# Mamba-2 block with a LoRA feed-forward layer: x's transposes, D-skip, the decay scan and the layer norm get other places in their engines' order

## Chip, cores and metric

One core of one Trainium2 chip runs the whole program in one launch. The metric is the device time of that launch in microseconds (us); lower is better. The engines are TensorE (PE; PEld is its weight load), VectorE (DVE), ScalarE (ACT), GpSimd (POOL) and SyncE (SP), whose queue issues the DMAs. Everything is float32.

## The reference, cut to what matters

x is 2048 tokens by 1024 channels. It is normalised, goes through a state-space layer and through a linear layer with a routed LoRA, and both results are added to it.

```python
xn = layernorm(x)                                   # over 1024 channels
proj = xn @ in_proj_w.T                             # gate 4096 | hbc 6144 | dt 64
conv = conv_bias + sum(pad[:, k:k+L] * conv_weight[:, k] for k in range(4))   # of hbc
xBC = silu(conv)                                    # x: 64 heads x 64, B and C: 8 groups x 128
dt_p = softplus(dt + dt_bias);  dA = exp(dt_p * -exp(A_log))
state = state * dA + dt_p * x (outer) B             # token by token
y = state . C + x * D                               # "D-skip"
y = y * rsqrt(mean(y*y over a group of 512) + eps) * norm_weight * silu(gate)
out = x + y @ out_proj_w.T + (xn @ W_base.T + b_base + top-2 LoRA of xn)
```

## The kernel before

All matrices have channels on partitions. The kernel works in three stages:

- **Fill** (about 0 to 195 us). The layer norm of the first 1024 tokens (`ln_first`), the small projections, dt and the decays (`small`), and the first products of `in_proj`.
- **Loop** (about 195 to 2130 us). 32 blocks b: two halves s of 1024 tokens (b 0 to 15 and 16 to 31), in each 8 groups g, in each two times 512 tokens. A block has four chunks c = 0 to 3 of 128 tokens; one chunk is one *slot* of the loop at line 1115. In every slot the state-space scan of one chunk is woven into the products of `in_proj`.
- **Rest** (2130 us to the end). The gate, the norm's scale and `out_proj`.

A *product* is 8 matmuls of 128x512 (one of seven products of a pair of weight tiles, in the manner of Strassen). `products(n, side)` (line 657) takes n of them from a stream and, after each, does an equal share of a list of small steps. TensorE's instructions keep the order in which the program issues them. So do, among themselves, those given to `pin` (line 96): each is put behind the last one pinned, on VectorE. All other instructions of VectorE and most of ScalarE's are ordered by the compiler's scheduler, which lets an instruction go ahead as soon as it believes that its inputs are there; ScalarE's moves (L740), xdd (L825), silu (L707, L723) and squares (L901) are held in program order. At run time each engine takes its instructions strictly as ordered.

A slot (lines 1115 to 1227) runs: first product with its steps; `scan_b` of this chunk; first step of `scan_a` of the *next* chunk; second product with its steps; second step of `scan_a`; third product with its steps; a fourth product in some slots; last step of `scan_a`. The four lists of steps are `parts[0]` to `parts[3]`. What matters of it:

- `scan_b` (834). TensorE: 16 matmuls **ps_y** (8 heads, each 64 rows of a bank) that take the mask product `dab` and the tokens' x as weights, and add to what ScalarE has put there; 8 matmuls **ps_e** (state times C); 2 matmuls **ps_st** from **xdd**. VectorE: `ecp` = ecp * ps_e (L863), y into `xg` = ecp + ps_y (L864), the state's sum (L878), all pinned. GpSimd scales the state (L85).
- `scan_a` (782), for the next chunk. Step 1: the decay scan `es` on VectorE (L791, pinned; one buffer, which xdd of the chunk before still reads). Step 2: TensorE's `ps_cb` (C times B, and B transposed), ScalarE's copies `cbm` and `bt` (L803, L805), then the **D-skip** (L812): four ScalarE instructions that write x * D into the bank of ps_y, once VectorE has read it for the chunk before (L864); then the **mask product** `dab` = es * cbm on VectorE (L817). Step 3: **xdd** on ScalarE, 8 instructions (L825).
- `conv` (694): ten steps for the next block. Per part (two tiles) one on ScalarE and two of three VectorE instructions each (L717, pinned). In c = 0, 1 and 2 the first three go into `parts[1]`, the second three into `parts[2]`.
- `turned` (729), x by token for the next block, in two times (k = 0, 1) 17 steps: 16 **moves** of 32 partitions on ScalarE (L740) and then one **transpose** of the whole on VectorE (L746) with the multiplication by dt (L753), both pinned. k = 0 serves chunks 0 and 1, k = 1 chunks 2 and 3. The steps per slot and list are in line 1163; the transposes come in `parts[1]` of c = 3 (k = 0) and of c = 1 (k = 1).
- `ln_next` (274), the layer norm of the second half's tokens, in four pieces; a piece runs through the first eight slots of each three blocks of b 0 to 11. `small` (340) of the piece follows, a step a slot, at the head of `parts[2]`. Their VectorE instructions are not pinned.
- In the second half, in c = 1, GpSimd adds the sums of the output weights (`out_sums`, four instructions at L85, named wo); VectorE does others of them in c = 3 (L938).

Before the loop, lines 1081 to 1092 do `conv` of block 0 beside 14 products, then the first 17 steps of `turned`, then `scan_a` of the first chunk.

Of the kernel before, what the change touches and what calls it, by code (L numbers as in the profile page):

```python
# [10 lines left out]
ALU = mybir.AluOpType  # L11
AX = mybir.AxisListType
# [3 lines left out]
H = 64  # L16
# [27 lines left out]
def mamba_lora_kernel(  # L44
# [229 lines left out]
    def ln_next(s, i):  # L274
# [9 lines left out]
        nc.vector.tensor_tensor(a, flat[:, 0:2, :], flat[:, 2:4, :], ALU.add)  # L284
        nc.vector.tensor_tensor(b, flat[:, 4:6, :], flat[:, 6:8, :], ALU.add)
        nc.vector.tensor_tensor(a, a, b, ALU.add)
        of = [a[:, 0, :], a[:, 1, :]]
# [4 lines left out]
        yield  # L292
        total = scratch("lsq")
        for h in range(2):
# [12 lines left out]
        for h in range(2):  # L307
            normal(flat[:, 4 * h : 4 * h + 4, :], std, ALU.mult)
            yield
# [4 lines left out]
        t4, t2 = (ev.tile([P, KH, Q], F32, tag="ev", name=f"t_{s}_{i}_{j}") for j in (4, 2))  # L314
        nc.vector.tensor_tensor(t1, b12, b11, ALU.subtract)
        nc.vector.tensor_tensor(t2, b22, t1, ALU.subtract)
        nc.vector.tensor_tensor(t4, b21, t2, ALU.subtract)
        t3 = ev.tile([P, KH, Q], F32, tag="ev", name=f"t_{s}_{i}_3")
        nc.vector.tensor_tensor(t3, b22, b12, ALU.subtract)
        yield  # L320
# [12 lines left out]
    def small(s, i, chunks, sm, home):  # L333
# [8 lines left out]
        def tile(what, shape):  # L342
# [10 lines left out]
        nc.vector.scalar_tensor_tensor(u, dt, -1.0, dt, ALU.mult, ALU.max)  # L353
        nc.scalar.activation(u, u, AF.Exp, scale=-1.0)
        nc.vector.tensor_scalar(dt, dt, 0.0, None, ALU.max)
        yield
        nc.vector.tensor_scalar(u2, u, 2.0, None, ALU.add)
        nc.vector.reciprocal(u2, u2)
        nc.vector.tensor_tensor(u, u, u2, ALU.mult)
        nc.vector.tensor_tensor(u2, u, u, ALU.mult)  # L360
        nc.vector.tensor_scalar(po, u2, 1.0 / 19.0, None, ALU.mult)
        for k in range(8, 0, -1):
            nc.vector.scalar_tensor_tensor(po, po, 1.0 / (2 * k + 1), u2, ALU.add, ALU.mult)
        nc.vector.scalar_tensor_tensor(po, po, 1.0, u, ALU.add, ALU.mult)
        dts = dt_of[s][:, chunks, :]
        nc.vector.scalar_tensor_tensor(dts, po, 2.0, dt, ALU.mult, ALU.add)

        at, ex = tile("at", [P, nch, H]), tile("ex", [P, nch, H])
        nc.vector.tensor_tensor(at, dts, na.unsqueeze(1).to_broadcast([P, nch, H]), ALU.mult)
        nc.scalar.activation(ex, at, AF.Exp)  # L370
# [29 lines left out]
        for c in range(nch):  # L400
            nc.vector.tensor_tensor_scan(
                run[:, c, :], da[:, c, :], zero.to_broadcast([H, Q]), 1.0, ALU.mult, ALU.add
            )


        nc.vector.memset(da[:, :, 0:1], 0.0)
        da_d = dram.tile([nch, H, Q], F32, tag=f"da_d_{n}", name=f"da_d_{n}")
# [11 lines left out]
        def best(src, name):  # L419
            m = lp.tile([P, nch, 1], F32, tag=f"m_{name}", name=f"m_{name}_{n}")  # L420
            nc.vector.tensor_reduce(m, src, AX.X, ALU.max)
            oh = lp.tile([P, nch, NE], F32, tag=f"oh_{name}", name=f"oh_{name}_{n}")
            nc.vector.tensor_tensor(oh, src, m.to_broadcast([P, nch, NE]), ALU.is_equal)
            nc.vector.tensor_tensor(oh, oh, rank_b, ALU.mult)
            f = lp.tile([P, nch, 1], F32, tag="first", name=f"first_{name}_{n}")
            nc.vector.tensor_reduce(f, oh, AX.X, ALU.max)
            nc.vector.tensor_tensor(oh, oh, f.to_broadcast([P, nch, NE]), ALU.is_equal)
# [4 lines left out]
        nc.vector.scalar_tensor_tensor(rest, oh1, -3.0e38, lg, ALU.mult, ALU.add)  # L432
        m2, oh2 = best(rest, "b")
        nc.vector.tensor_tensor(m2, m2, m1, ALU.subtract)
        nc.scalar.activation(m2, m2, AF.Exp)
        yield
        nc.vector.tensor_scalar(m1, m2, 1.0, None, ALU.add)
        nc.vector.reciprocal(m1, m1)
        nc.vector.tensor_scalar(m1, m1, SCALING, None, ALU.mult)
        nc.vector.tensor_tensor(m2, m2, m1, ALU.mult)  # L440
        nc.vector.tensor_tensor(oh1, oh1, m1.to_broadcast([P, nch, NE]), ALU.mult)
        nc.vector.tensor_tensor(oh2, oh2, m2.to_broadcast([P, nch, NE]), ALU.mult)
        nc.vector.tensor_tensor(oh1, oh1, oh2, ALU.add)
        for c in range(nch):
            hv = sm[:, c, H + NE :].rearrange("p (e r) -> p e r", r=RANK)
            nc.vector.tensor_tensor(
                hv, hv, oh1[:, c, :].unsqueeze(2).to_broadcast([P, NE, RANK]), ALU.mult
            )
# [222 lines left out]
    def steps(gen, n):  # L671

        return [lambda: next(gen, None) for _ in range(n)]
# [108 lines left out]
    def scan_a(s, g, half, c):  # L782
# [23 lines left out]
        if put_sums:  # L806
            put_sums()

        psy = ps_one.tile([P, 4, Q], F32, tag="y", name=f"ps_y_{n}")
        for j in range(4):  # L810
# [3 lines left out]
            )  # L814
        ms = dab
        masked[:] = [
            nc.vector.tensor_tensor(  # L817
                ms, es, cbm.unsqueeze(1).to_broadcast([P, HG, Q]), ALU.mult
            )
        ]  # L820
        yield
# [1025 lines left out]
```

## Time and profile before

| what | us |
|---|---|
| three runs, median (lowest to highest) | 3426.97 (3425.16 to 3427.97) |
| the profiled execution, its own time | 3425.95 |
| its span, first to last instruction | 3424.2 |
| TensorE busy in the span | 3316.1 |
| VectorE, ScalarE, GpSimd busy | 2564.5, 1674.2, 701.5 |
| mean granted TensorE clock | 0.989 |

The profile is of one execution. A line of a timeline gives the start, the duration, the engine, the line of the kernel, the operation, what it writes <- what it reads, the shapes and the count; in square brackets stands the engine's idle time before it and whose work ended it. Durations of matmuls include their way through the array, so that neighbours overlap: 8 matmuls of 128x512 show as 3.60 us and follow each other every 3.43. In a list of waits a line reads: engine, tile and line that waited, <- whom for, us in total, times, the longest.

The typical slot holds three products and lasts 13.6 to 14.05 us if TensorE does not wait; one with four lasts 17.0 to 17.5.

### The profile page before, as it was taken

The numbers are of one execution on the slowest core, as the hardware profiler recorded it, in microseconds if no ns is written. First come the engines' busy times: TensorE is split into PE (matmuls) and PEld (weight loads), VectorE is DVE, ScalarE is ACT, GpSimd is POOL, SyncE is SP. The second block draws the span as 40 slices with busy tenths as digits, with TensorE's granted clock in tenths as the row PEclk, the third lists the DMA queues.
The fourth block names the chain that finished last, engine by engine and source line by source line (L and its number), as shares of the span: only waits on it lengthen the run. The fifth ranks groups of instructions, "written<-read, shape, count | busy, mean of one in ns | idle before, by whom it ended". The sixth has DMA issues, their size and how long they took to land.

```text
span 3424.2 us, 40725 instructions
## 1 busy us (share of the span) xinstructions
PE 3316.1 (97%) x13509; PEld 2163.9 (63%) x13509; DVE 2564.5 (75%) x2873; ACT 1674.2 (49%) x4014; POOL 701.5 (20%) x483
## 2 busy tenths in 40 slices
PE   9989999999999999999999999999999999999999
PEld 7445554554554454455445545688888788888888
DVE  7378878988868889898878886477877666556554
ACT  2267776787686677777687765222222200000000
POOL 4122222222200021121212121355655100000000
PEclk9999999999999999999999999999999999999999
DMA  7546565665588988999888889578777887585644
GB/s 254 188 149 212 191 215 174 198 214 189 191 288 293 317 277 288 290 283 286 256 257 267 258 270 299 181 262 286 263 258 263 286 307 244 193 303 185 213 163 147
DMA packets 550818, 826.69 MB, mean 241 GB/s; under 512 B 36688, under 2 KB 266320, under 8 KB 547024
## 3 DMA queue, kind: packets, MB, share of 16 engines
q1 hardware_dynamic: 550608, 824.08, 73.2%
q8 instruction: 108, 1.77, 0.2%
q14 instruction: 102, 0.84, 0.1%
HBM read 564.88 MB, written 259.06 MB: 241 GB/s over the span
## 4 chain that ended last, share of the span: by engine, by line
PE 67%; DVE 15%; ACT 8%; DMA 6%; issue 3%; SPq 1%; POOL 0%; DVEq 0%; ACTq 0%; POOLq 0%
PE ps_x_w L81 8%; PE ps_x_x L81 8%; PE ps_x_z L81 6%; PE ps_a_w L81 5%; PE ps_y_w L81 5%; PE ps_a_x L81 5%; PE ps_y_x L81 5%; PE ps_a_z L81 4%; PE ps_y_z L81 4%; DVE xg L717 3%; ACT x_blocks L740 3%; PE ps_e L81 2%; PE ps_y L81 2%; DVE es L791 2%; PE ps_x_b L81 2%
## 5 line engine op out<-in xcount | busy, mean ns | idle before, releaser
L740 ACT COPY x_blocks<-xg 32x256 f32<-32x256 f32 x1024 | 411.5, 402 | 15.1 <-DVE x_by_token L746 0.9
L85 POOL TENSOR_TENSOR state<-state,tot 128x512 f32<-128x512 f32 x112 | 133.0, 1187 | 1104.8 <-PE ps_e L81 960.6
L717 DVE SCALAR_TENSOR_TENSOR xg<-raw_x,cw,xg 128x512 f32<-128x512 f32 x384 | 337.1, 882 | 15.0 <-ACT xg L710 9.9
L825 ACT ACTIVATE xdd<-x_by_token,es 128x64 f32<-128x64 f32 x1024 | 259.7, 335 | 114.6 <-DVE x_by_token L753 110.2
L81 PE MATMUL ps_x_w<-t,w 128*128 128x256 f32 x1344 | 305.1, 380 | 0.0
L791 DVE TENSOR_TENSOR_SCAN es<-dab,here 128x1024 f32<-128x1024 f32 x128 | 296.1, 2314 | 8.7 <-DMA dab<-da_d 4.7
L81 PEld LDWEIGHTS ps_x_w<-t,w 128*128 128x128 f32 x1344 | 256.3, 191 | 42.6 <-issue 8.0
L812 ACT ACTIVATE ps_y<-xg,dsk 128x128 f32<-128x128 f32 x512 | 189.0, 369 | 111.7 <-DVE xg L864 91.2
L1784 ACT COPY ps_x_w<-ps_a_w 128x512 f32<-128x512 f32 x28 | 16.0, 570 | 419.6 <-PE ps_a_w L81 419.6
L81 PEld LDWEIGHTS ps_y<-dab,x_by_token 128*64 128x64 f32 x2048 | 113.9, 140 | 157.4 <-issue 142.0
L81 PE MATMUL ps_a_w<-q,w 128*128 128x256 f32 x896 | 204.1, 381 | 2.5 <-DMA w<-w 2.5
L81 PE MATMUL ps_y<-dab,x_by_token 128*64 128x128 f32 x2048 | 144.9, 285 | 58.9 <-DVE x_by_token L753 30.2
L81 PEld LDWEIGHTS ps_a_w<-q,w 128*128 128x128 f32 x896 | 171.2, 191 | 26.4 <-DMA w<-w 2.9
L81 PE MATMUL ps_x_x<-op_again,s_x 128*128 128x512 f32 x384 | 175.6, 600 | 3.0 <-ACT s_x L533 2.0
L863 DVE TENSOR_TENSOR ecp<-ecp,ps_e 128x512 f32<-128x512 f32 x120 | 81.9, 683 | 127.6 <-PE ps_e L81 123.9
L81 PE MATMUL ps_a_x<-op_again,a_x 128*128 128x512 f32 x384 | 173.3, 594 | 0.0
L81 PE MATMUL ps_y_x<-op_again,s_x 128*128 128x512 f32 x384 | 173.1, 593 | 0.0
L81 PE MATMUL ps_x_x<-op,s_x 128*128 128x512 f32 x368 | 169.1, 603 | 3.2 <-ACT s_x L533 3.2
L717 DVE SCALAR_TENSOR_TENSOR bc<-raw_b,cw,bc 128x512 f32<-128x512 f32 x192 | 157.6, 829 | 17.9 <-ACT bc L710 14.8
L81 PE MATMUL ps_y_x<-op,s_x 128*128 128x512 f32 x368 | 169.1, 603 | 0.0
L817 DVE TENSOR_TENSOR dab<-es,cbm 128x1024 f32<-128x1024 f32 x128 | 158.4, 1237 | 14.1 <-ACT cbm L803 13.8
L81 PE MATMUL ps_a_x<-op,a_x 128*128 128x512 f32 x368 | 165.8, 593 | 0.0
(326 smaller groups left out, 6630.8 us busy)
## 6 DMA issues: line engine op xcount, KB each, us to landing
w<-w SPq DMA_DIRECT2D x196, 512.0 KB, 3.8
dab<-da_d SPq DMA_DIRECT2D x128, 512.0 KB, 6.0
w<-wo SPq DMA_DIRECT2D x112, 448.0 KB, 4.8
raw<-ev SPq DMA_DIRECT2D x192, 256.0 KB, 3.5
a_x<-in_w_in_dram SPq DMA_DIRECT2D x168, 256.0 KB, 4.5
ecp<-run_d SPq DMA_DIRECT2D x256, 128.0 KB, 5.1
y<-xg SPq DMA_DIRECT2D x64, 512.0 KB, 5.7
gy<-y SPq DMA_DIRECT2D x64, 512.0 KB, 6.5
```

The source lines that it names most:

```text
L81: tc.keep_in_program_order(nc.tensor.matmul(*args, **kw))
L85: ins = nc.gpsimd.tensor_tensor(*args)
L717: ins = nc.vector.scalar_tensor_tensor(dst[:, i, :], raw[:, i, k : k + TB], cw[:, ti, k : k + 1], dst[:, i, :], ALU.mult, ALU.add,)
L740: ins = nc.scalar.copy(blocks[32 * b : 32 * b + 32, :, :, i, :].rearrange("p c j r -> p j c r"), x[32 * i : 32 * i + 32, :, 2 * k : 2 * k ...
L791: ins = nc.vector.tensor_tensor_scan(es.rearrange("p h t -> p (h t)"), dab.rearrange("p h t -> p (h t)"), here, 0.0, ALU.mult, ALU.add,)
L812: nc.scalar.activation(psy[:, j, :], xg[:, j, cs], AF.Copy, scale=dsk[:, at : at + 1])
L817: nc.vector.tensor_tensor(ms, es, cbm.unsqueeze(1).to_broadcast([P, HG, Q]), ALU.mult)
L825: ins = nc.scalar.activation(xdd[:, h, :], xdt[:, h, :], AF.Copy, scale=es[:, h, Q - 1 : Q])
L863: pin(nc.vector.tensor_tensor(ecp, ecp, pse, ALU.mult))
L1784: nc.scalar.copy(px, pa)
```

## The change

Five edits:

1. `turned` keeps its 34 steps per block but spreads them anew (table `TURN`): in c = 2, 0, 4, 4, 4 steps for the four lists (before 0, 3, 4, 3); in c = 3, 4, 0, 1, 3 (before 3, 4); in c = 0 as before 2, 3, 3, 2; in c = 1, 3, 0, 1, 0 (before 3, 4). The moves of a k end with `parts[0]` of c = 3 or c = 1, and the transpose comes with `parts[2]`, behind the conv steps of that list.
2. In `scan_a` the mask product stands ahead of the D-skip, and a `yield` parts them: the D-skip comes after the third product instead of the second.
3. The decay scan (first step of `scan_a`) is issued ahead of `scan_b` instead of behind it.
4. The VectorE instructions of `ln_next` and `small` are pinned (`chain`), so that they stand in one order with conv, transposes and sums. In `ln_next` the additions of squares move behind later work, and there are two more `yield`s; the steps per slot follow.
5. The 14 last products of the fill also take the first 17 steps of `turned`; only three are left behind them.

```diff
+    class Chained:
+
+        def __getattr__(self, name):
+            call = getattr(nc.vector, name)
+            return lambda *args, **kw: pin(call(*args, **kw))
+
+    chain = Chained()
...
-    def normal(part, by, alu):
+    def normal(part, by, alu, engine=nc.vector):
-        nc.vector.tensor_tensor(
+        engine.tensor_tensor(
...
         total = scratch("lsq")
+        sqs = []
+
+        def add_up(*pairs):
+            for a, b in pairs:
+                chain.tensor_tensor(a, a, b, ALU.add)
+
         for h in range(2):
-            normal(flat[:, 4 * h : 4 * h + 4, :], mean, ALU.subtract)
+            normal(flat[:, 4 * h : 4 * h + 4, :], mean, ALU.subtract, chain)
+            if sqs:
+                add_up((total, sqs.pop()))
             for k in (4 * h, 4 * h + 2):
                 sq = ev.tile([P, 2, 2 * Q], F32, tag="ev", name=f"lsq_{s}_{i}_{k}") if k else total
                 nc.scalar.activation(sq, flat[:, k : k + 2, :], AF.Square)
                 if k:
-                    nc.vector.tensor_tensor(total, total, sq, ALU.add)
+                    sqs.append(sq)
             yield
+        add_up((total, sqs[0]), (total, sqs[1]))
+        yield
         ps = over_channels([total[:, 0, :], total[:, 1, :]], "aux", f"var_{s}_{i}")
         std = lp.tile([P, 2 * Q], F32, tag="lnstd", name=f"std_{s}_{i}")
         nc.scalar.activation(std, ps, AF.Sqrt, bias=eps, scale=1.0 / DM)
-        nc.vector.reciprocal(std, std)
+        yield
+        chain.reciprocal(std, std)
         yield
...
+        ms = dab
+        masked[:] = [
+            nc.vector.tensor_tensor(
+                ms, es, cbm.unsqueeze(1).to_broadcast([P, HG, Q]), ALU.mult
+            )
+        ]
+        yield
         psy = ps_one.tile([P, 4, Q], F32, tag="y", name=f"ps_y_{n}")
         for j in range(4):
             at = 4 * g + j
             nc.scalar.activation(
                 psy[:, j, :], xg[:, j, cs], AF.Copy, scale=dsk[:, at : at + 1]
             )
-        ms = dab
-        masked[:] = [
-            nc.vector.tensor_tensor(
-                ms, es, cbm.unsqueeze(1).to_broadcast([P, HG, Q]), ALU.mult
-            )
-        ]
         yield
...
-    products(14, steps(conv(*blocks[0]), 10))
+    turn = turned(*blocks[0])
+    c1, m1 = steps(conv(*blocks[0]), 1), steps(turn, 1)
+    products(14, (c1 * 6 + [lambda: None] + (c1 + m1 * 2) * 4 + m1 * 9))
...
-    turn = turned(*blocks[0])
-    for _ in range(17):
+    for _ in range(3):
         next(turn)
...
+    TURN = (2, 3, 3, 2), (3, 0, 1, 0), (0, 4, 4, 4), (4, 0, 1, 3)
...
-            side += steps(ln, {2: 1, 3: 1, 4: 1, 5: 2, 6: 1}.get(at, 0))
+            side += steps(ln, {2: 1, 3: 2, 4: 1, 5: 3, 6: 1}.get(at, 0))
...
-                for p, k in zip(parts, ((2, 3, 3, 2), (3, 4), (0, 3, 4, 3), (3, 4))[c]):
+                for p, k in zip(parts, TURN[c]):
                     p += steps(turn, k)
             products(1, parts[0])
+            next(a, None)
             scan_b(*blk, c)
...
             if second:
                 load_decays(*second)
-            next(a, None)
...
             products(1, parts[1])
             next(a, None)
             products(1, parts[2])
+            next(a, None)
             products(min(n - 3, 1), parts[3])
             next(a, None)
             do_put_off()
```

Left out are the lines in `ln_next` and `small` that only say `chain.` for `nc.vector.`.

More of the change, by code (lines that the diff above doesn't have):

```diff
@@ L283, in ln_next @@
         b = ev.tile([P, 2, 2 * Q], F32, tag="ev", name=f"half_{s}_{i}")
-        nc.vector.tensor_tensor(a, flat[:, 0:2, :], flat[:, 2:4, :], ALU.add)
-        nc.vector.tensor_tensor(b, flat[:, 4:6, :], flat[:, 6:8, :], ALU.add)
-        nc.vector.tensor_tensor(a, a, b, ALU.add)
+        chain.tensor_tensor(a, flat[:, 0:2, :], flat[:, 2:4, :], ALU.add)
+        chain.tensor_tensor(b, flat[:, 4:6, :], flat[:, 6:8, :], ALU.add)
+        chain.tensor_tensor(a, a, b, ALU.add)
         of = [a[:, 0, :], a[:, 1, :]]
@@ L293, in ln_next @@
         total = scratch("lsq")
+        sqs = []
+        def add_up(*pairs):
+            for a, b in pairs:
+                chain.tensor_tensor(a, a, b, ALU.add)
         for h in range(2):
-            normal(flat[:, 4 * h : 4 * h + 4, :], mean, ALU.subtract)
+            normal(flat[:, 4 * h : 4 * h + 4, :], mean, ALU.subtract, chain)
+            if sqs:
+                add_up((total, sqs.pop()))
             for k in (4 * h, 4 * h + 2):
@@ L304, in ln_next @@
         nc.scalar.activation(std, ps, AF.Sqrt, bias=eps, scale=1.0 / DM)
-        nc.vector.reciprocal(std, std)
+        yield
+        chain.reciprocal(std, std)
         yield
         for h in range(2):
-            normal(flat[:, 4 * h : 4 * h + 4, :], std, ALU.mult)
+            normal(flat[:, 4 * h : 4 * h + 4, :], std, ALU.mult, chain)
             yield
@@ L314, in ln_next @@
         t4, t2 = (ev.tile([P, KH, Q], F32, tag="ev", name=f"t_{s}_{i}_{j}") for j in (4, 2))
-        nc.vector.tensor_tensor(t1, b12, b11, ALU.subtract)
-        nc.vector.tensor_tensor(t2, b22, t1, ALU.subtract)
-        nc.vector.tensor_tensor(t4, b21, t2, ALU.subtract)
+        chain.tensor_tensor(t1, b12, b11, ALU.subtract)
+        chain.tensor_tensor(t2, b22, t1, ALU.subtract)
+        chain.tensor_tensor(t4, b21, t2, ALU.subtract)
         t3 = ev.tile([P, KH, Q], F32, tag="ev", name=f"t_{s}_{i}_3")
-        nc.vector.tensor_tensor(t3, b22, b12, ALU.subtract)
+        chain.tensor_tensor(t3, b22, b12, ALU.subtract)
         yield
@@ L349, in small @@
         dt, u, u2, po = (tile(w, [P, nch, H]) for w in ("dtp", "u", "u2", "po"))
-        nc.vector.tensor_tensor(
+        chain.tensor_tensor(
             dt, sm[:, :, 0:H], dtb.unsqueeze(1).to_broadcast([P, nch, H]), ALU.add
         )
-        nc.vector.scalar_tensor_tensor(u, dt, -1.0, dt, ALU.mult, ALU.max)
+        chain.scalar_tensor_tensor(u, dt, -1.0, dt, ALU.mult, ALU.max)
         nc.scalar.activation(u, u, AF.Exp, scale=-1.0)
-        nc.vector.tensor_scalar(dt, dt, 0.0, None, ALU.max)
+        chain.tensor_scalar(dt, dt, 0.0, None, ALU.max)
         yield
[L357 to L361, printed above, removed]
+        chain.tensor_scalar(u2, u, 2.0, None, ALU.add)
+        chain.reciprocal(u2, u2)
+        chain.tensor_tensor(u, u, u2, ALU.mult)
+        chain.tensor_tensor(u2, u, u, ALU.mult)
+        chain.tensor_scalar(po, u2, 1.0 / 19.0, None, ALU.mult)
         for k in range(8, 0, -1):
-            nc.vector.scalar_tensor_tensor(po, po, 1.0 / (2 * k + 1), u2, ALU.add, ALU.mult)
-        nc.vector.scalar_tensor_tensor(po, po, 1.0, u, ALU.add, ALU.mult)
+            chain.scalar_tensor_tensor(po, po, 1.0 / (2 * k + 1), u2, ALU.add, ALU.mult)
+        chain.scalar_tensor_tensor(po, po, 1.0, u, ALU.add, ALU.mult)
         dts = dt_of[s][:, chunks, :]
-        nc.vector.scalar_tensor_tensor(dts, po, 2.0, dt, ALU.mult, ALU.add)
+        chain.scalar_tensor_tensor(dts, po, 2.0, dt, ALU.mult, ALU.add)
         at, ex = tile("at", [P, nch, H]), tile("ex", [P, nch, H])
-        nc.vector.tensor_tensor(at, dts, na.unsqueeze(1).to_broadcast([P, nch, H]), ALU.mult)
+        chain.tensor_tensor(at, dts, na.unsqueeze(1).to_broadcast([P, nch, H]), ALU.mult)
         nc.scalar.activation(ex, at, AF.Exp)
@@ L400, in small @@
         for c in range(nch):
-            nc.vector.tensor_tensor_scan(
+            chain.tensor_tensor_scan(
                 run[:, c, :], da[:, c, :], zero.to_broadcast([H, Q]), 1.0, ALU.mult, ALU.add
             )
-        nc.vector.memset(da[:, :, 0:1], 0.0)
+        chain.memset(da[:, :, 0:1], 0.0)
         da_d = dram.tile([nch, H, Q], F32, tag=f"da_d_{n}", name=f"da_d_{n}")
@@ L420, in best @@
             m = lp.tile([P, nch, 1], F32, tag=f"m_{name}", name=f"m_{name}_{n}")
-            nc.vector.tensor_reduce(m, src, AX.X, ALU.max)
+            chain.tensor_reduce(m, src, AX.X, ALU.max)
             oh = lp.tile([P, nch, NE], F32, tag=f"oh_{name}", name=f"oh_{name}_{n}")
-            nc.vector.tensor_tensor(oh, src, m.to_broadcast([P, nch, NE]), ALU.is_equal)
-            nc.vector.tensor_tensor(oh, oh, rank_b, ALU.mult)
+            chain.tensor_tensor(oh, src, m.to_broadcast([P, nch, NE]), ALU.is_equal)
+            chain.tensor_tensor(oh, oh, rank_b, ALU.mult)
             f = lp.tile([P, nch, 1], F32, tag="first", name=f"first_{name}_{n}")
-            nc.vector.tensor_reduce(f, oh, AX.X, ALU.max)
-            nc.vector.tensor_tensor(oh, oh, f.to_broadcast([P, nch, NE]), ALU.is_equal)
+            chain.tensor_reduce(f, oh, AX.X, ALU.max)
+            chain.tensor_tensor(oh, oh, f.to_broadcast([P, nch, NE]), ALU.is_equal)
             return m, oh
@@ L431, in small @@
         rest = lp.tile([P, nch, NE], F32, tag="rest", name=f"rest_{n}")
-        nc.vector.scalar_tensor_tensor(rest, oh1, -3.0e38, lg, ALU.mult, ALU.add)
+        chain.scalar_tensor_tensor(rest, oh1, -3.0e38, lg, ALU.mult, ALU.add)
         m2, oh2 = best(rest, "b")
-        nc.vector.tensor_tensor(m2, m2, m1, ALU.subtract)
+        chain.tensor_tensor(m2, m2, m1, ALU.subtract)
         nc.scalar.activation(m2, m2, AF.Exp)
         yield
[L437 to L443, printed above, removed]
+        chain.tensor_scalar(m1, m2, 1.0, None, ALU.add)
+        chain.reciprocal(m1, m1)
+        chain.tensor_scalar(m1, m1, SCALING, None, ALU.mult)
+        chain.tensor_tensor(m2, m2, m1, ALU.mult)
+        chain.tensor_tensor(oh1, oh1, m1.to_broadcast([P, nch, NE]), ALU.mult)
+        chain.tensor_tensor(oh2, oh2, m2.to_broadcast([P, nch, NE]), ALU.mult)
+        chain.tensor_tensor(oh1, oh1, oh2, ALU.add)
         for c in range(nch):
             hv = sm[:, c, H + NE :].rearrange("p (e r) -> p e r", r=RANK)
-            nc.vector.tensor_tensor(
+            chain.tensor_tensor(
                 hv, hv, oh1[:, c, :].unsqueeze(2).to_broadcast([P, NE, RANK]), ALU.mult
@@ L814, in scan_a @@
             )
-        ms = dab
-        masked[:] = [
-            nc.vector.tensor_tensor(
-                ms, es, cbm.unsqueeze(1).to_broadcast([P, HG, Q]), ALU.mult
-            )
-        ]
         yield
```

## The prediction

> **What bounds the kernel now.** I read the page first, then who waited for whom, then the timelines of two places. The page shows one engine that is never out of work:
>
> ```profile
> PE 3316.1 (97%) x13509; PEld 2163.9 (63%) x13509; DVE 2564.5 (75%) x2873; ACT 1674.2 (49%) x4014; POOL 701.5 (20%) x483
> ```
>
> TensorE is the bound, so an edit is worth what it takes from, or adds to, TensorE's idle time. Everything that changes lies before 2130 us: the fill (0 to 195) and the loop (195 to 2130). TensorE's own waits in the loop, in the list of waits cut to that window, are the whole pot:
>
> ```profile
> PE ps_y L81 <- DVE x_by_token L753: 30.2, 15, 3.4
> PE ps_st L81 <- ACT xdd L825: 14.9, 13, 3.3
> PE ps_y L81 <- issue: 10.3, 7, 2.2
> PE ps_y L81 <- DMA raw<-ev: 7.0, 1, 7.0
> ```
>
> (us, times, longest.) So 62 us go by in front of ps_y and its kin: mostly because x by token (transpose L746, times dt L753) is late, and a quarter because xdd, ScalarE's last work of a slot, is. On TensorE's timeline I took the time ahead of the first ps_y of every slot: slots c=2 (which need the x of the second transpose, made in c=1) lose 43 us, 27 in the first half (b 0 to 15) and 16 in the second; c=0, 1 and 3 together 10. The other engines' waits in the same window tell what the change is aimed at:
>
> ```profile
> DVE ecp L863 <- PE ps_e L81: 123.9, 54, 6.9
> ACT ps_y L812 <- DVE xg L864: 91.2, 59, 4.1
> DVE x_by_token L746 <- ACT x_blocks L740: 50.7, 26, 5.4
> ```
>
> VectorE idles ahead of its first sum, ScalarE ahead of D-skip, VectorE ahead of the transpose; none of these engines is the bound, so these microseconds count only where TensorE waits at their end.
>
> **1. First moves in the fill.** TensorE's timeline at the end of the fill, and ScalarE's line beside it:
>
> ```profile
> 176.20 3.60 PE L81 MATMUL ps_a_x<-op,a_x 128*128 128x512 f32 x8
> 188.56 1.98 PE L81 MATMUL ps_y<-dab,x_by_token 128*64 128x128 f32 x16 [8.76 <-DVE dab L817]
> 190.47 2.08 PE L81 MATMUL ps_st<-xdd,bt 128*128 128x512 f32 x2
> 192.33 4.82 PE L81 MATMUL ps_y_x<-op,s_x 128*128 128x512 f32 x8
> ```
>
> ```profile
> 175.76 6.59 ACT L740 COPY x_blocks<-xg 32x256 f32<-32x256 f32 x16
> ```
>
> Sixteen moves, 1.26 us of transpose, a 2.30 us scan and a 1.24 us mask run one after the other while TensorE idles 8.76 us; ps_y, ps_st and ps_y_x then take 8.88 us, against 1.09, 1.02 and 3.60 (5.71) for the same groups at 1728, because the granted clock is 0.82 over 172 to 200. The change puts the 16 moves and the first transpose beside the last products. ScalarE has gaps of 9.75, 3.31 and 2.9 us there, so they are covered. What is late next: three moves (1.2), cbm and bt (0.4), then the mask (1.23) beside four D-skips (1.5): from 175.86 that ends by 179.0, before ps_a_x ends at 179.80. So the gap goes whole and the clock with it: -8.76 - 3.17 = **-11.9 us**. Without that cover at most the 6.59 us of moves come back.
>
> The Trainium skill, TensorE: Matmul & The Clock Gate (Terms), prices throttled time as that time times the share not granted. With the row's 0.82 over 28 us that is 5.0 us, and the term would be -13.8; I stay with the three groups' rows, since part of the slow clock fell on an idle TensorE.
>
> **2. D-skip one product on.** The same 512 instructions of 0.37 us, but no longer at the head of ScalarE's queue waiting 91.2 us for xg (L864): behind them stood moves and xdd, and for xdd ps_st waits 14.9. Bounds: 0 to -14.9. A late xdd has other causes too (ScalarE is busy 13.4 of 14 us in the slot at 1728, and c=2 gets two more moves of 0.40), so half: **-7.5**. D-skip now stands just ahead of the last moves and of xdd's 2.02, so ps_y gets it some 2 us before it is due.
>
> **3. Transposes a product later.** In c=3 the moves now end a product before their transpose; VectorE's 50.7 us of waiting goes. c=3 has no conv steps, so x by token is then in time for c=0. Of the 10 us ahead of ps_y in c=0, 1 and 3 I take **-6** (bounds 0 and -10).
>
> In c=1 the same shift costs. VectorE there, in block 25 (slot from 1742.42), and GpSimd beside it:
>
> ```profile
> 1744.64 0.69 DVE L863 TENSOR_TENSOR ecp<-ecp,ps_e 128x512 f32<-128x512 f32 x1 [0.58 <-PE ps_e L81]
> 1745.36 0.69 DVE L864 TENSOR_TENSOR xg<-ecp,ps_y 128x512 f32<-128x512 f32 x1
> 1745.97 0.68 DVE L878 TENSOR_TENSOR state<-state,ps_st 128x512 f32<-128x512 f32 x1
> 1746.56 2.28 DVE L791 TENSOR_TENSOR_SCAN es<-dab,here 128x1024 f32<-128x1024 f32 x1
> 1748.76 5.04 DVE L717 SCALAR_TENSOR_TENSOR xg<-raw_x,cw,xg 128x512 f32<-128x512 f32 x3
> 1753.73 1.23 DVE L746 STREAM_TRANSPOSE x_by_token<-x_blocks 128x1024 f32<-128x1024 f32 x1
> 1754.89 1.18 DVE L817 TENSOR_TENSOR dab<-es,cbm 128x1024 f32<-128x1024 f32 x1
> 1756.00 1.21 DVE L753 TENSOR_TENSOR x_by_token<-x_by_token,dt 128x1024 f32<-128x1024 f32 x1
> ```
>
> ```profile
> 1747.97 6.98 POOL L85 TENSOR_TENSOR wo<-wo 128x512 f32<-128x512 f32 x4 [2.24 <-DMA s_x<-s_x_d]
> ```
>
> No idle time at all from ecp on, and x by token ends 1757.21 where TensorE was ready at 1756.10. The moves were done long before: there is no wait to remove here. In the new order the second three conv steps stand ahead of the transpose (both are in the third product's list, conv first, and VectorE's chain keeps the order). I lay it out with the start-to-start times of these rows. The scan may start when xdd has read es, at 1743.85: 2.20. Sums 0.72, 0.61, 0.59: 1747.97. Three conv steps beside GpSimd 5.05, mask 1.13, three conv steps 2.3 (those of 1741.74 took 2.32), transpose 1.16, times dt 1.21: 1758.8, **1.6 us later**. If the mask falls under GpSimd too it is 2.5 (the longest x by token of the same size took 2.30 for 1.21); if the scan can start at once at 1742.42, 0.2. I take 1.6 for the ten second-half slots c=2 that wait over 0.25 us now (b17, 19, 21, 22, 24, 25, 27 to 30): **+16**. In b18, where c=1 has no GpSimd adds, the same sum gives 13.5 us against a slot of 13.6: the others cost nothing.
>
> The row is that conv steps take 1.68 us beside GpSimd's adds and 0.75 alone. The Trainium skill, SBUF — State Buffer (SBUF: two separate sides), makes it an exclusive lock held for a whole instruction, which speaks against this change: a fourth add would hold the mask for about 1 us more. By that rule it is +26 and the forecast 3426.5.
>
> **4. Decay scan ahead of the sums.** Nothing is added. The scan uses idle time of VectorE (123.9 us), but it now waits for xdd, and behind it in VectorE's queue stand both sums and the state, for which D-skip and the next ps_e wait. xdd ends 0.1 to 2.2 us after ps_y in nearly every slot, where ps_e ends at 2.22; three slots with 4.2 to 4.4 would hold the sums 2 us, with 8 us to spare. Its worth is already in the start at 1743.85. No price of its own: 0, between -5 and +6.
>
> **5. Layer norm and small() in the chain.** First half only: the same instructions, two additions later. Today they float ahead of ecp and wait there (std for ScalarE 7.9, scr 15.5, lsq 7.4). That goes, but reciprocal (1.75) and one multiplication (1.57) now stand in c=1 ahead of the transpose in b1, 4, 7 and 10, and so do small()'s sixteen short steps in b2, 5, 8 and 11. Laid out like above, x by token moves by -0.6 to +2.4. Against it the one 7.0 us wait (b14, an ev that went ahead of ecp) may not recur. I take **0** for the first half's 27 us in c=2, bounds -27 and +30. The 7 transfers that ln_next issues, and load_decays', keep their slots: SP's queue is as before.
>
> **Sum:** -11.9 - 7.5 - 6 + 16 + 0 = -9.4. The profiled execution took 3425.95 (span 3424.2 and 1.75 around it), 1.0 under the median of 3426.97, so 3416.5.
>
> **Rivals.** *The chain of c=1 starts earlier too.* If ScalarE, freed of 91 us of waiting, has xdd done at the slot's start, the +16 shrinks to about 0, xdd's waits go nearly whole (-12), and the first half gains some (-6): -11.9 - 12 - 6 - 6 = -36, 3390. For it: VectorE's idle time shrinks everywhere. Against: ScalarE is full in c=0, where this xdd is made.
>
> *Slower: the conv steps ahead of the transpose.* Nothing is won at the chain's start, and each of the 21 slots c=2 that wait now waits 2.2 us more (three conv steps), the other 11 half a us: 46 + 5.5 - 11.9 - 13.5 = +26, 3452. It decides from 0.8 us a block on (25.4 / 32), below the 1.6 of my own layout. For it: eight VectorE rows without a gap. Against: in the first half much of what stands in front today floats.
>
> *The fill does not pay:* the moves there wait for conv, which waits for raw_b, and the gap stays for the most part; with +2 from the rest: 3428.
>
> **Chances.** About 0.2% (7 us) is what a measurement can tell. Forecast (3403 to 3430) 0.45, of which 0.28 faster and 0.17 the same; 3390 case 0.25; slower 0.20; no fill 0.10 (0.06 the same, 0.04 slower). Faster 0.53, same 0.23, slower 0.24. The range leaves 0.08 below and 0.12 above: 3385 to 3445.
>
> **What would show it.** Right: no gap over 1 us on TensorE between 176 and 195, clock 1.0 there; L746 without waits for L740; L812 without waits for L864; in block 25 c=1 x by token ends some 16 us after ps_y and the next ps_y waits 2 to 3. Wrong: ps_y waits in c=2 of under 20 us in all (the 3390 case) or over 70 (the slower one); es waiting for xdd by more than 1 us a slot; a gap left at 180.

## The result and the profile after

The changed kernel takes **3482.16 us** (median of four runs, 3479.59 to 3483.31) beside 3427.47 (3425.16 to 3428.17) of the kernel before, run on the same chip: a ratio of 1.016, 95% interval [1.0142, 1.0177]. It is slower by 54.7 us, 37 above the upper end of the range. The profiled execution has a span of 3481.5 us (before 3424.2) and a mean granted clock of 0.983 (0.989).

The engine line of the page after:

```profile
PE 3323.3 (95%) x13509; PEld 2173.8 (62%) x13509; DVE 2573.1 (74%) x2873; ACT 1690.8 (49%) x4028; POOL 732.9 (21%) x483
```

TensorE does the same 13509 matmuls and is busy 7 us longer, in a span 57 us longer: most of the loss is idle time. TensorE's waits in the loop, cut to 195 to 2200 us:

```profile
PE ps_y L81 <- DVE x_by_token L771: 71.9, 18, 9.3
PE ps_y L81 <- issue: 27.7, 9, 5.8
PE ps_st L81 <- ACT xdd L844: 9.4, 9, 2.8
```

Nearly as many waits for x by token as before (18 against 15), but each 4.0 us long instead of 2.0. Waits put down to "issue" can be of the same kind: one is taken apart below, and there x by token had ended 0.1 us before. By slots, the time ahead of the first ps_y in c=2 went from 28.3 to 76.6 us in the first half and from 17.6 to 32.6 in the second; in c=0, 1 and 3 (but for the very first slot) it fell from 18.3 to 10.5. This counts from the start of the matmul before, less 0.43 us, so that a slot without any wait still adds 0.09; in the idle times that the profile prints, the three are 26.0 to 74.0, 15.4 to 30.3 and 8.7 to 1.3, and the 27, 16 and 10 of the prediction are nearer to these. Measured from one first ps_y to the next, the fill and the first slot are 11.1 us shorter, the rest of the first half is 46.4 us longer (c=1 +37.3, c=2 +20.8, c=0 and 3 -11.8), the second half 20.4.

VectorE's and ScalarE's waits in the same window:

```profile
DVE es L809 <- ACT xdd L844: 126.2, 64, 8.3
DVE dab L829 <- ACT cbm L821: 82.6, 56, 7.0
DVE ecp L882 <- PE ps_e L81: 47.4, 27, 7.6
DVE x_by_token L764 <- ACT x_blocks L758: 2.6, 2, 2.0
```

```profile
ACT ps_y L837 <- DVE xg L883: 166.9, 76, 8.0
```

The transposes no longer wait for their moves (50.7 before), as edit 1 says. VectorE's idle time ahead of its first sum did not go; it changed its name, from 123.9 us for ps_e to 47.4 for ps_e and 126.2 for xdd. And ScalarE's wait at D-skip, which edit 2 was to shorten, grew from 91.2 to 166.9. The place of the scan is a part of that: in the change without edit 3 (run below) it is 126.4.

The end of the fill:

```profile
174.10 3.60 PE L81 MATMUL ps_a_x<-op,a_x 128*128 128x512 f32 x8
180.51 1.09 PE L81 MATMUL ps_y<-dab,x_by_token 128*64 128x128 f32 x16 [2.81 <-DVE dab L829]
181.54 1.13 PE L81 MATMUL ps_st<-xdd,bt 128*128 128x512 f32 x2
```

The gap of 8.76 us is 2.81, and ps_y takes 1.09 us instead of 1.98.

**Where the first half lost it.** Block 8, c=1, first ps_y at 721.33. VectorE:

```profile
720.69 2.29 DVE L809 TENSOR_TENSOR_SCAN es<-dab,here 128x1024 f32<-128x1024 f32 x1 [0.19 <-ACT xdd L844]
...
724.08 0.68 DVE L882 TENSOR_TENSOR ecp<-ecp,ps_e 128x512 f32<-128x512 f32 x1
...
725.99 2.32 DVE L735 SCALAR_TENSOR_TENSOR xg<-raw_x,cw,xg 128x512 f32<-128x512 f32 x3
728.23 1.29 DVE L117 TENSOR_SCALAR scr<-scr 128x128 f32<-128x128 f32 x1
...
732.40 2.90 DVE L117 SCALAR_TENSOR_TENSOR scr<-scr 128x128 f32<-128x128 f32 x9
735.34 1.24 DVE L117 SCALAR_TENSOR_TENSOR dt<-scr 128x128 f32<-128x128 f32 x1
736.62 1.31 DVE L117 TENSOR_TENSOR at<-dt,na 128x128 f32<-128x128 f32 x1
737.85 2.31 DVE L735 SCALAR_TENSOR_TENSOR xg<-raw_x,cw,xg 128x512 f32<-128x512 f32 x3
740.07 1.24 DVE L764 STREAM_TRANSPOSE x_by_token<-x_blocks 128x1024 f32<-128x1024 f32 x1
...
741.80 1.22 DVE L771 TENSOR_TENSOR x_by_token<-x_by_token,dt 128x1024 f32<-128x1024 f32 x1
```

and TensorE behind it:

```profile
743.12 1.98 PE L81 MATMUL ps_y<-dab,x_by_token 128*64 128x128 f32 x16 [4.68 <-issue]
745.03 2.08 PE L81 MATMUL ps_e<-bc,state 128*128 128x128 f32 x8
746.90 1.91 PE L81 MATMUL ps_st<-xdd,bt 128*128 128x512 f32 x2
```

Ahead of the transpose stand, in this order, scan, sums, three conv steps, small()'s short steps (728.23 to 737.9 with the mask between them) and three more conv steps. x by token ends 21.7 us after ps_y; the slot lasts 21.79 (18.41 before). ScalarE's Exp of small() and its xdd, in the same slot:

```profile
737.96 0.31 ACT L388 ACTIVATE ex<-at 128x128 f32<-128x128 f32 x1 [4.48 <-DVE at L117]
743.05 2.02 ACT L844 ACTIVATE xdd<-x_by_token,es 128x64 f32<-128x64 f32 x8 [2.88 <-DVE x_by_token L771]
```

The Exp is done long before x by token, so what is late here is VectorE's chain alone. And TensorE pays twice: after the 4.68 us it runs ps_y, ps_e and ps_st in 1.98, 2.08 and 1.91 us where they take 1.09, 1.16 and 1.02 in the undisturbed slot at 193.22.

small() goes on in the next block: nine short steps of the router stand ahead of the transpose in c=1 of b 3, 6, 9 and 12, where before the change none did. In b 12 (ps_y at 992.98, x by token 5.4 us later than before) the first of them and the transpose are:

```profile
1002.56 0.16 DVE L117 TENSOR_SCALAR m_a<-m_b 128x2 f32<-128x2 f32 x1
1007.43 1.24 DVE L764 STREAM_TRANSPOSE x_by_token<-x_blocks 128x1024 f32<-128x1024 f32 x1
```

TensorE's idle time ahead of ps_y in c=2 of the first half, by what stands in c=1 of the block (the second conv steps stand ahead of the transpose in all of them after the change):

| blocks | in c=1 after the change | before, us | after | after, small() not pinned (run below) |
|---|---|---|---|---|
| 2, 5, 8, 11 | small()'s sixteen steps | 6.7 | 23.8 | 5.8 |
| 3, 6, 9, 12 | small()'s router steps | 0.5 | 11.9 | 0.9 |
| 1, 4, 7, 10 | layer norm | 9.2 | 22.2 | 22.1 |
| 0, 13, 14, 15 | neither | 9.7 | 16.0 | 14.6 |

### The profile page after: what moved, and what is told of

Read it like the earlier page. It is cut to its first block, busy times and chain, and to the rows that moved or that the text cites. A ratio compares the mean times of both kernels' runs of the same rounds, so it can differ in the third digit from the quotient of the medians.

```text
span 3481.5 us, 40686 instructions
## 1 busy us (share of the span) xinstructions
PE 3323.3 (95%) x13509; PEld 2173.8 (62%) x13509; DVE 2573.1 (74%) x2873; ACT 1690.8 (49%) x4028; POOL 732.9 (21%) x483
## 4 chain that ended last, share of the span: by engine, by line
PE 77%; DVE 10%; ACT 6%; issue 3%; DMA 3%; SPq 0%; POOL 0%; DVEq 0%; ACTq 0%; POOLq 0%
PE ps_x_x L81 10%; PE ps_x_w L81 8%; PE ps_a_x L81 7%; PE ps_y_x L81 6%; PE ps_x_z L81 6%; PE ps_a_w L81 5%; PE ps_y_w L81 5%; PE ps_a_z L81 4%; PE ps_y_z L81 4%; DVE xg L735 3%; PE ps_e L81 3%; PE ps_y L81 3%; PE ps_st L81 2%; PE ps_x_b L81 2%; ACT x_blocks L758 2%
## 5 line engine op out<-in xcount | busy, mean ns | idle before, releaser
L85 POOL TENSOR_TENSOR state<-state,tot 128x512 f32<-128x512 f32 x112 | 179.7, 1604 | 1180.9 <-PE ps_e L81 1055.3
L837 ACT ACTIVATE ps_y<-xg,dsk 128x128 f32<-128x128 f32 x512 | 189.4, 370 | 198.4 <-DVE xg L883 166.9
L81 PE MATMUL ps_y<-dab,x_by_token 128*64 128x128 f32 x2048 | 151.9, 294 | 108.4 <-DVE x_by_token L771 71.9
L81 PE MATMUL ps_e<-bc,state 128*128 128x128 f32 x960 | 153.6, 308 | 0.0
```

Of the source, the lines that this page charges most:

```text
L81: tc.keep_in_program_order(nc.tensor.matmul(*args, **kw))
L85: ins = nc.gpsimd.tensor_tensor(*args)
L837: nc.scalar.activation(psy[:, j, :], xg[:, j, cs], AF.Copy, scale=dsk[:, at : at + 1])
```

## The experiments

Two theories stand in the first expectations. **Theory 1:** the second three conv steps ahead of the transpose in c=1 are the loss in both halves. **Theory 2:** they are the loss in the second half only; in the first it is the pinned layer norm and small(), which stand ahead of the transpose too. A third suspect is the scan ahead of the sums: it waits for xdd, and sums, D-skip and xdd follow late. All numbers below are against the kernel before, timed beside each; "alone" is the kernel before with one edit.

**Single edits.** The fill, edit 5, alone:

```diff
-    products(14, steps(conv(*blocks[0]), 10))
+    turn = turned(*blocks[0])
+    c1, m1 = steps(conv(*blocks[0]), 1), steps(turn, 1)
+    products(14, (c1 * 6 + [lambda: None] + (c1 + m1 * 2) * 4 + m1 * 9))
...
-    for _ in range(17):
-        next(turn)
```

> The kernel before with edit 5 alone: the first 17 steps of turned go beside the last 14 products of the fill. Both theories: TensorE's first ps_y comes 8 us earlier and the second 11 us earlier, as in the changed kernel, and nothing later moves: about 3416 us, -11. If the fill's gain is lost again in the loop, 3427.

Measured: 3416.72 against 3425.63, ratio 0.9972 [0.9962, 0.9981]. The fill pays 8.9 us of the 11 expected. Edit 1 alone:

```diff
-    for _ in range(17):
+    for _ in range(20):
...
-                for p, k in zip(parts, ((2, 3, 3, 2), (3, 4), (0, 3, 4, 3), (3, 4))[c]):
+                for p, k in zip(parts, ((2, 3, 3, 2), (3, 0, 1, 0), (0, 4, 4, 4), (4, 0, 1, 3))[c]):
```

> The kernel before with edit 1 alone: the new table of steps, with 20 steps of turned behind the fill. Theory 1 (the conv steps ahead of the transpose in c=1 are the loss in both halves): slots c=2 wait some 45 us more, and with the slow clock after it the time is 3427 + 45 = 3472. Theory 2 (the first half's loss is the pinned layer norm and small(), which stand ahead of the transpose): only the second half loses, 3427 + 15 = 3442.

Measured: 3531.64 against 3425.63, ratio 1.0312 [1.0294, 1.0329]: +106 us, twice the whole change and far above both theories' numbers. Both halves lose, as Theory 1 says. In c=1 of the second half, times dt ends 17.7 us after ps_y on average (before 14.7) and the slots c=1 take 43 us more in all. So edit 1 is the large cost, and the rest of the change takes half of it back. Edit 2 alone (the mask product goes ahead of the D-skip, with a `yield` between):

```diff
             products(1, parts[2])
+            next(a, None)
             products(min(n - 3, 1), parts[3])
```

> The kernel before with edit 2 alone: the mask ahead of the D-skip, the D-skip a step later. If the later place frees ScalarE, its waits for xg (L864) fall from 91 us to under 30 and the time by some 7 us, 3419. If the scheduler puts the unpinned D-skip back where its input is ready, the waits stay near 91 us and the time at 3426.

Measured: 3409.38 against 3420.9, ratio 0.9968 [0.9958, 0.9978]: -11.5 us, though ScalarE still waits 100 us at D-skip, so neither case foreseen; ps_st's waits for xdd fell from 14.9 to 10.7 us, and by which way the rest of the gain comes is not shown. Edit 3 alone:

```diff
             products(1, parts[0])
+            next(a, None)
             scan_b(*blk, c)
...
-            next(a, None)
             if c in (1, 3):
```

> The kernel before with edit 3 alone: the decay scan ahead of scan_b. What is to be told apart: if the scan only trades VectorE's wait for ps_e (124 us) for a wait for xdd, the chain of c=1 starts no earlier and the time stays within 7 us of 3426. If it starts up to 2 us earlier in c=1, slots c=2 wait less: 3412. If it holds the sums back and D-skip with them: 3440, with ScalarE's waits for xg well above 91 us.

Measured: 3440.02 against 3420.9, ratio 1.0053 [1.0037, 1.007]: +19.1 us, the last of the three cases, with ScalarE's waits for xg at 195.2 us. Edit 4 alone, all the lines of `ln_next` and `small` in this manner, with the two yields:

```diff
-        nc.vector.tensor_tensor(a, a, b, ALU.add)
+        chain.tensor_tensor(a, a, b, ALU.add)
```

> The kernel before with edit 4 alone: ln_next and small pinned, the transposes where they were. Theory 1: within 10 us of before, 3417 to 3437. Theory 2: the first half loses 25 us or more, 3452.

Measured: 3447.19 against 3425.63, ratio 1.0064 [1.0049, 1.0079]: +21.6 us, all in the first half, nearer to Theory 2. Yet there the idle time ahead of ps_y in c=2 fell, from 26.0 to 15.2 us; what rose is ps_st's waiting for xdd, from 11.5 to 34.0. The sum of the five alone is +126, the change +55.

**One edit taken out of the change.** Edit 1 out (the old tuples; the fill then does all 17 steps):

```diff
-    TURN = (2, 3, 3, 2), (3, 0, 1, 0), (0, 4, 4, 4), (4, 0, 1, 3)
+    TURN = (2, 3, 3, 2), (3, 4), (0, 3, 4, 3), (3, 4)
```

> The changed kernel without edit 1: the table of steps as before, edits 2 to 5 stay. Theory 1: the loss goes whole, 3482 - 60 or more: at most 3422. Theory 2: only the second half's 15 us come back, 3467. If the scan ahead of the sums (edit 3) is what costs, it stays near 3470 too, and the scan's waits for xdd stay at 100 us or more.

Measured: 3465.42 against 3425.63, ratio 1.0123 [1.0107, 1.0139]. Edit 1, +106 alone, is worth only +15 on top of the others: Theory 2's number, and near the one for the scan, so this run does not part these two. Edit 4 out:

```diff
-        chain.tensor_tensor(a, a, b, ALU.add)
+        nc.vector.tensor_tensor(a, a, b, ALU.add)
```

> The changed kernel without edit 4: ln_next and small float again. chain_only lost 25 us in the first half and nothing in the second, so if that adds to the rest it is 3482 - 25 = 3457; if the first half's whole loss of 46 us comes from the pinned instructions standing ahead of the transpose in c=1, 3436. If the transposes' place alone makes the first half's loss, it stays near 3480.

Measured: 3458.98 against 3420.9, ratio 1.0107 [1.0092, 1.0123]. Edit 4 costs +17 in the change, near to what it cost alone. Edit 3 out:

```diff
             products(1, parts[0])
-            next(a, None)
             scan_b(*blk, c)
...
                 load_decays(*second)
+            next(a, None)
```

> The changed kernel without edit 3: the decay scan is issued behind scan_b again. The single edits add up to +126 us, the change is +55. Theory A: the difference is edit 3. With edit 1 alone the scan starts 4.2 us after ps_y in c=1 of the second half and times dt ends at 17.7; in the change it starts at -0.3 and times dt ends at 15.8. Without edit 3 the c=1 slots therefore lose about 2 us each again, 50 us or more over both halves: 3530 or more. Theory B: edit 3 costs its 19 us in the change as it does alone, and the edits fail to add for another reason: 3463.

Measured: 3530.27 against 3425.39, ratio 1.0311 [1.0294, 1.0328]: +105. TensorE's and VectorE's first waits, same window:

```profile
PE ps_y L81 <- DVE x_by_token L771: 102.8, 19, 8.9
PE ps_y L81 <- issue: 45.6, 10, 7.7
```

```profile
DVE ecp L882 <- PE ps_e L81: 258.0, 95, 12.6
```

Theory A holds. Without edit 3 VectorE idles 258 us ahead of its sums, with the scan (2.3 us) still to be done behind them, and x by token ends as late as with edit 1 alone (17.75 us after ps_y in the second half). Edit 3, a loss alone, takes back 50 us of edit 1: the scan falls as the account of the change's loss.

**The order in c=1.** In the change, and then with edit 1 alone:

```diff
-    TURN = (2, 3, 3, 2), (3, 0, 1, 0), (0, 4, 4, 4), (4, 0, 1, 3)
+    TURN = (2, 3, 3, 2), (3, 1, 0, 0), (0, 4, 4, 4), (4, 0, 1, 3)
```

> The changed kernel with one figure of the table changed: in c=1 the transpose and the multiplication by dt stand in the second product's list again, ahead of the second three conv steps (3, 1, 0, 0), and all moves and c=3 stay as in the change. If the conv steps ahead of it are what delays x by token, c=1 gains 2.2 us a slot where it binds: the second half loses its 20 us and the first half 30: 3432. If the start of the chain or the pinned instructions bind, at most 10 us come back: 3472.

Measured: 3452.9 against 3420.9, ratio 1.0087 [1.0072, 1.0102]: 22.7 us of the change's 54.7 are gone. In the second half times dt now ends 12.3 us after ps_y (15.8 in the change) and c=2 waits 2.0 us in all instead of 32.6. In the first half c=1 gained 59 us, but c=2 lost 34. The total lies between the two numbers foreseen.

> The kernel before with edit 1, but with the steps of c=1 as 3, 1, 0, 0: the transpose of c=1 stays in the second product's list, ahead of the second three conv steps; c=2 and c=3 have the new table. Edit 1 whole took 106 us (3531.64 against 3425.63). Theory A: all of that is the second conv steps ahead of the transpose in c=1, which put the end of times dt from 14.7 to 17.7 us after ps_y in the second half. Then this kernel is within 8 us of the kernel before, or up to 6 us faster, since c=3's transpose no longer waits for moves. Theory B: the moves packed into c=2 and c=3 cost by themselves (ScalarE is full there, and xdd comes later): at least 30 us of the 106 stay, 3457 or more.

Measured: 3426.48 against 3426.35, ratio 1.0004 [0.9992, 1.0016]. All 106 us of edit 1 are one step in one of its four tuples: the transpose of c=1 in the third list instead of the second. The moves' new places in c=2 and c=3 cost nothing, and win nothing.

**small().** It is what c=2 lost there. The kernel before, with `small` pinned alone:

```diff
-        nc.vector.tensor_scalar(u2, u, 2.0, None, ALU.add)
+        chain.tensor_scalar(u2, u, 2.0, None, ALU.add)
```

> The kernel before with only the small() part of edit 4: its VectorE steps pinned, the layer norm's not. With both pinned the time rose by 21.6 us (3447.19 against 3425.63), and the slots c=2 of b 2, 5, 8 and 11, which carry small(), alone took 35.7 us longer. Theory A: the loss is small()'s own. Its chain of some sixteen short VectorE steps now waits behind the transpose and its times dt, ScalarE's Exp of small() waits for them, xdd stands behind that Exp in ScalarE's order, and TensorE's ps_st behind xdd. Then this kernel loses about 35 us or more: near 3462, with those four slots at 24 us or more. Theory B: pinning as such costs, for the layer norm's instructions as for these: about half of the 21.6 us, near 3438, with the four slots at some 20 us.

Measured: 3445.71 against 3426.35, ratio 1.0065 [1.005, 1.008]: +19.4, nearer to B's total, by A's mechanism. The four slots c=2 of b 2, 5, 8 and 11 take 23.4, 25.2, 22.9 and 26.5 us (16.1, 14.5, 14.6, 17.9 before: +34.8); slots c=1 and c=0 gave back 12. In the first half ps_st waits 38.1 us for xdd (11.5 before). ScalarE in b 5, in this kernel, and TensorE beside it:

```profile
544.62 1.28 ACT L377 ACT_TABLE_LOAD   x1
550.47 0.31 ACT L377 ACTIVATE ex<-at 128x128 f32<-128x128 f32 x1 [4.57 <-DVE at L117]
550.69 1.04 ACT L908 ACTIVATE sq<-xg 128x1024 f32<-128x1024 f32 x1
551.63 2.00 ACT L832 ACTIVATE xdd<-x_by_token,es 128x64 f32<-128x64 f32 x8
```

```profile
553.69 2.07 PE L81 MATMUL ps_st<-xdd,bt 128*128 128x512 f32 x2 [7.61 <-ACT xdd L832]
555.55 5.49 PE L81 MATMUL ps_a_x<-op,a_x 128*128 128x512 f32 x8
```

x by token had ended at 543.50, so xdd could have run then; it stands behind small()'s Exp, which waits for the last of the short steps. In the kernel before, xdd ran at 543.91 in this block. The change with the same lines of `small` back at `nc.vector`:

> The changed kernel with small() unpinned; the layer norm stays pinned, all else as in the change. Without edit 4 whole the change gave 3458.98, 23 us less than the 3482.16 of the change. Theory A: small() is all of that: 3459, within 6. Theory B: the change's c=1 slots are already the late ones, so the layer norm's reciprocal and multiplication in front of their transpose cost there too, though they cost nothing without edit 1: about half, 3470.

Measured: 3450.47 against 3425.39, ratio 1.0075 [1.006, 1.009]: 30 us less than the change, more than edit 4 whole (17) and than either theory said. So small() is all of edit 4's loss, and the layer norm's part looks like a gain of some 13 us beside it (8.5 by the two times as they stand; the two intervals just miss each other).

**Both undone:** that, and `(3, 1, 0, 0)` for c=1 in `TURN`.

> The changed kernel with two things undone: the steps of c=1 as 3, 1, 0, 0 (transpose ahead of the second conv steps, as before), and small() unpinned. Left are the new places of the moves in c=2 and c=3 (about 0 by themselves), the D-skip, the scan ahead of the sums, the layer norm's part of edit 4 and the fill. Theory A: what is left costs what the scan costs alone, 19 us, on top of edits 2 and 5 (3397 to 3406): about 3420. Theory B: the scan ahead of the sums is only bad where ScalarE's D-skip comes at its old place; with the D-skip a product later it is free or a gain, 3400 or less. A value of 3440 or more would say that a third cause is missing.

Measured: 3419.79 against 3425.39, ratio 0.9984 [0.9974, 0.9993]. Theory A's number. The two together were 60 us: more than the change's whole loss, and more than c=1's order (22.7) and small() (29.6) undone singly. With the transpose alone put early, small()'s cost moves to c=2: there, in b 2, 5, 8 and 11 of that run, TensorE idles 22.6 us (0.0 in the change), in three of the four for the norm's squares, in one for xdd.

**What is left: edits 2 and 5, and the place of the scan.** The diffs of edits 2 and 5 above in one kernel, and then with `chain` in `ln_next` alone:

> The kernel before with edits 2 and 5 alone (D-skip a product later, first moves in the fill). By themselves they took off 11.5 and 8.9 us. Theory A: they act in different places (the loop and the fill) and add: about 20 us off, 3406 beside 3426. Theory B: both only give back the same late moves or the same late xdd, and together they bring no more than the better of them: 3414.

Measured: 3397.0 against 3426.35, ratio 0.9923 [0.9897, 0.995]; the profiled spans differ by 24.5. The interval (17 to 35 us off) holds Theory A's 20, so the two add, and this is the version to keep.

> Edits 2 and 5, and of edit 4 the layer norm's part alone (ln_next pinned, with its two more yields; small() not). Theory A (the loss of edit 4 is small()'s): the layer norm's part is a gain of 10 to 14 us, what the c=1 slots of the first half gained with edit 4 alone (11.7): 3393 to 3397, where edits 2 and 5 alone give some 3406. Theory B (pinning as such costs): about 11 us above edits 2 and 5 alone, 3417.

Measured: 3400.52, ratio 0.9933 [0.9916, 0.995]: the same within the intervals. The layer norm pinned is neither the gain nor the loss foreseen here; if it gains, then only in the change.

The scan ahead of `scan_b` only where c is 1, and only where it is not (`!=`), each with edits 2 and 5:

```diff
+            if c == 1:
+                next(a, None)
             scan_b(*blk, c)
...
-            next(a, None)
+            if not (c == 1):
+                next(a, None)
```

> Edits 2 and 5, and the decay scan ahead of scan_b only in the slots c=1 (in the others behind it, as before). In c=1 VectorE's chain is what the next ps_y waits for, and there the scan runs in VectorE's idle time ahead of the sums. Theory A: this is the part that pays: about 16 us less than edits 2 and 5 alone (what c=1 of the second half gained with the scan ahead in all slots), near 3383. Theory B: in c=1 the scan's wait for xdd puts off sums and state, and what is won at the transpose is lost at the next slot's start: within 6 us of 3397, or above.

> The complement: edits 2 and 5, and the scan ahead of scan_b in c=0, 2 and 3 only. Theory A: here the move costs, since in these slots no chain of VectorE is late, while the scan's wait for xdd puts off the sums, and D-skip, moves and the next xdd on ScalarE behind them: 25 us or more above edits 2 and 5 alone, 3422 or more. Theory B: the cost is not in the place of the scan: within 8 us of 3397.

Measured: scan_c1 3397.19 against 3421.12, ratio 0.992 [0.99, 0.994]; scan_not_c1 3444.17, ratio 1.0059 [1.0038, 1.0079]. In c=1 the move is free, and its 6 us of gain at the last slot of the loop (-31.2 against -25.5 for edits 2 and 5) are no difference in the times. In c=0, 2 and 3 it costs 47 us by the profiled spans (3446.2 against 3399.7) on top of edits 2 and 5; the first half's c=2 alone lost 22 of them. VectorE's sums start 1.7 to 2.1 us later there on average (6.0, 5.9 and 4.2 us after ps_y in c=0, 2 and 3, from 3.9, 4.0 and 2.6). TensorE's waits are spread: those for xdd, "issue" and the norm's squares together rise by some 20 us against edits 2 and 5, those for x by token hardly. Which of them carries the loss is not settled, nor why the scan ahead in *all* slots (two_undone: 18 us on edits 2 and 5 by the spans, 24 by the times) costs less than in three of four.

## Why the prediction was wrong, by its steps

| step | predicted | measured |
|---|---|---|
| 1 fill | -11.9 | -8.9 alone; -11.1 by the second slot in the change |
| 2 D-skip | -7.5 | -11.5 alone |
| 3 c=0, 1, 3 | -6 | -7.8 in their waits |
| 3 c=1, second half | +16 | +15.0 in c=2's waits; 23.5 of time (undoing both) |
| 4 scan | 0 (-5 to +6) | +19 alone; +18 to +24 in two_undone; -50 beside edit 1's order |
| 5 first half | 0 (-27 to +30) | +48 in c=2's waits; 39 of time (undoing both) |

- **Right in sign:** the fill and the D-skip (together -29.4, or -24.5 by the spans, for -19.4 foreseen; one fell short, the other went beyond). The fill left 2.81 us of gap where none was foreseen: one move stood behind an `ev` until 173.79, so that the transpose began at 174.22. The D-skip's way was not the one foreseen: its waits for xg were to go and stayed at 100 us.
- **Right in part by luck:** the second half, +15 where +16 was said. In the ten blocks that were counted, x by token came 1.1 us later where 1.6 was laid out, and the waits rose by 9.9 us; the other 5.0 are b18 and b31, which were to cost nothing. In block 25 itself the scan began 1.8 us ahead of ps_y and not 1.4 behind it, and x by token ended 15.1 us after ps_y (14.8 before), where 16.4 was laid out. The Trainium skill's lock (SBUF — State Buffer, SBUF: two separate sides) made the term +26, by a fourth add that holds one more step for about 1 us. One more step was indeed held there: beside the four adds the conv steps took 0.94, 1.64, 1.64 and 1.75 us, the next one 0.75. So the +15 does not speak against that rule.
- **The step that failed is step 5, the 0 for the first half.** The prediction laid out -0.6 to +2.4 us for x by token, set it off against waits of floating instructions that would go, and took the middle. It moved by +2.9 on average (16.05 to 18.97; +0.4 to +5.4 by blocks), above the upper end of the layout. Sixteen times 2.9 is 47 us, and the waits in c=2 rose by 48: the first half began with c=2 already waiting, so that the delay was paid in full. Two things were wrong in the step. It counted small() in b 2, 5, 8 and 11 only; the router steps in b 3, 6, 9 and 12 had no term, and there x by token moved most (+4.6 us on average, +11.4 us of waits, gone again without small() pinned). And the set-off does not hold beside edit 1: with edit 4 alone c=2's waits did fall by 10.8 us, but with the transpose behind the second conv steps, small()'s steps come on top of them (29 us of the 48, by the table of blocks above).
- What stands behind small()'s *result* (the Exp on ScalarE, xdd behind it, then ps_st) had no term either. It is the loss of edit 4 alone, but not of the change, where ps_st waits 9.4 us for xdd (14.9 before).
- **Second, the scan "with no price of its own".** The prediction let the sums wait for xdd, but left out the scan's own 2.3 us between xdd and the sums, and gave them eight microseconds to spare. In c=0, 2 and 3 the sums came 1.7 to 2.1 us later, and the scan's place there cost 47 us (scan_not_c1). D-skip, which follows the sums, then waits 150 us in all instead of 100; that this is the way by which the loss reaches TensorE was not shown.
- **Third, a wait was priced at its own length.** See below: behind waits of 4 us and over TensorE also ran at half clock.
- The rival "slower: the conv steps ahead of the transpose" (3452, chance 0.20) had a part of the mechanism, and its own point of decision, 0.8 us a block, was under the layout's 1.6. The forecast kept away from it by the first half's 0. It took every wait from the conv steps, though, and gave small() no part. Waits of ps_y in c=2 "over 70 (the slower one)" were named as its mark: they are 109.

## What to carry to other kernels

When instructions go into a fixed order, list for each one what then stands behind it in its own queue, in every slot that carries it, and which engine waits for its *result* and what stands behind that waiter. In the change the cost was of the first kind (short steps and conv steps, then the transpose, then ps_y); with small() pinned alone it was of the second (Exp, then xdd, then ps_st). The pinned engine's busy time shows neither: VectorE's went from 2564.5 to 2573.1 us. Price an edit that lengthens a chain by the stage where that chain is already the last to end, in full, and don't offset it by a gain that holds only without the other edits. Edits that share a chain don't add: test each alone and each left out, since here one edit (the scan) cost 19 us alone, and saved 50 next to another.

## What the runs showed of the hardware

- **A long wait of TensorE is paid twice.** In the loop the granted clock falls to a half in stretches of 3.41, 6.83 or 10.24 us. After the change, 10 of TensorE's 11 idle times of 4 us or more end inside such a stretch and the last 0.1 us ahead of one, and none of 6 between 1.5 and 2 us; with edit 1 alone it is 17 of 18, the last 0.4 us ahead of one, and 0 of 6. In the loop these stretches come to 109 us after (48 before, 157 with edit 1 alone, 38 with edits 2 and 5). Half of the 61 us more is 31 us: the most that the clock can have added to the 57. It is why the c=2 slots of the first half are 20.8 us longer, though the wait itself falls into c=1: the half-clock time in them rose from 13.4 to 56.8 us, half of that rise is 21.7, and TensorE's idle time inside them went from 1.8 to 2.3 only. Slot by slot, too, the added time is half of the added half-clock time, within 0.6 us.
- The Trainium skill, TensorE: Matmul & The Clock Gate (Why this matters for your kernels), says to avoid idle gaps above about 3 us between bursts of matmuls. The trace agrees: of the 5 gaps of 3 to 4 us in the loop of the change one ends at half clock, and behind the other four a half-clock stretch begins 0.25 to 1.43 us later.
- A wait that the profile puts down to "issue" can be a real one: ps_y's 4.68 us in block 8 ended 0.1 us after x by token.
